# The last slot of an attention and convolution kernel: second pointwise layer and guides of one block as seven block products

## Chip, cores and metric

The kernel runs on one core of one Trainium2 chip. The metric is the device time of one execution in microseconds (us). TensorE (PE) multiplies matrices into PSUM, VectorE (DVE) does elementwise work and reads PSUM, ScalarE (ACT) does exponentials, GELU and copies, GpSimd (POOL) does small elementwise work, SyncE (SP) issues most DMAs.

## What is computed

The input x is 4 images of 64 x 64 pixels with 256 channels, float32. Layer 0 is full self-attention over the 4096 pixels of an image. Layer 1 is convolutional, cut to what matters here:

```python
perceived = depthwise_conv3x3(x, w_perc) + b_perc            # 256 -> 768 channels
hid = gelu(perceived @ w_up1.T + b_up1)                      # first pointwise layer, 768 -> 512
h   = x + hid @ w_up2.T + b_up2                              # second pointwise layer, 512 -> 256
q, k, v = split(h @ w_qkv.T + b_qkv)
scores = q . k over the 3 x 3 neighbours / 16
out = h + sum(softmax(scores) * v over the 3 x 3 neighbours)
```

The scores are formed without q and k: with G = Wq Wk (folded at the start), each pixel's "guide" is `g = G h + b`, and a score is `g . h` of the neighbour.

## The kernel before

**Slots and blocks.** An image is cut into 8 blocks of 8 rows (512 pixels); 4 images give 32 blocks. Slot s (0 to 31) does layer 0's attention of block s: 16 points (`points`, line 1091), each with one 1024-wide exponential on ACT (`weight`), four acc matmuls on PE (`product`, line 323, P times V), and one 1024-wide addition of the softmax denominator on DVE (`add_up`, line 337). At every even point PE also makes the next energies (`energy`, line 304, shown as e). Layer 1 follows behind: slot s also does the depthwise taps of block s − 2 and the pointwise layers, guides and scores of block k = s − 3, and the output of block a = s − 5. The last slot, 31, has more: k + 1 = 29 is done as well as k = 28, and the taps of blocks 29 and 30.

**The order** is written out by hand and each engine executes its instructions in that order. For every point: energies, the exponential, the jobs of `jobs[point]` (line 1129 in the last slot), `product`, `add_up`, and then a number of depthwise steps on DVE (`conv`, `tap_of` at line 477, one multiply-add of 128 x 512 each; the additions of line 483 make mixtures of the results). In the last slot these steps are spread evenly: 108 steps over 14 points, 7 or 8 each, with 20 at most by the end of point 2, so 11 in point 3. The first 60 belong to block 29 and end in point 7; its hidden layer (`hidden_part(k + 1, ...)`) starts in point 8.

**Seven products.** A product of a 2 x 2 block matrix with a 2 x 2 block matrix can be done with seven block products in place of eight, with additions before and behind (a Strassen form). The first pointwise layer does this for blocks 0 to 29 (`hidden_part`, tiles hid_a, hid_bc, hid_de, hid_gf). The second pointwise layer does it in `update_mix` (lines 669, 670: mixtures of hid), `update_part` (parts ab, cd, eg, f: 4 + 4 + 4 + 2 matmuls of 256 columns at line 534, with two DVE differences at lines 687 and 688 between ab and cd) and `gather` (lines 542 to 556: DVE adds each product into the result, ACT copies the first). Part f ends with four bias additions (line 698) and `guide_mix` (line 806). The guides do it in `guide_part` (2 + 2 + 2 + 1 matmuls, a DVE difference at line 833). The plain forms are `update(s, c)` (line 639, four matmuls of 512 columns, then two DVE operations at line 645, and with c = 1 the `border_terms`, lines 867 and 868) and `guide(s, i)` (line 783, two matmuls of 512 columns and one ACT operation at line 787).

Before, slots 3 to 30 use the seven products for update and guide; slot 31 uses the plain forms for blocks 28 and 29. The plain form of update needs the weights as they came, but the mixed weights stand in their place in `wup2`; so slot 31 starts with a DMA that loads that quarter again.

**PSUM banks.** A job takes its bank from `job_bank` (tag "m", two banks in turn): a job's first matmul waits until whoever reads the bank of the job before the previous one is done. Output tiles `o` have two buffers too; `lo` (block output, line 1029, with DVE at lines 1042 and 1054 and a DMA to HBM) and the two gmix tiles of `guide_mix` share them.

**The others in the slot:** `local_values` (lv, line 895, DVE 908), `scores` (s, line 936, ACT 956, POOL 961), `local_sum` (POOL 984), `local_total` (ld, line 998), `local_reciprocal` (DVE 1017), `border` (c, line 879). After slot 31 a tail starts with the denominators' matmul (dps, line 376) and does what is left of blocks 28 to 31.

## Time and profile before

| | us |
|---|---|
| time, median of 3 runs | 3453.34 (3453.23 to 3453.67) |
| the profiled execution, its own time | 3452.66 |
| its span, first to last instruction | 3450.8 |
| slot 31, from the dps before it (3199.97) to the dps behind it (3336.10) | 136.1 |
| the tail behind it | 114.7 |
| granted clock of TensorE | 0.999 |

The profile is one execution. "PE 3438.8 (100%)" is the busy time of an engine and its share of the span. The chain lists the work that ended last, followed back from the last instruction. A timeline row gives start, length, engine, line, operation, output <- inputs, how many were merged, and in brackets the idle time ahead of it and who ended it. A float32 matmul leaves two rows, so "x8" of 512 columns is four matmuls. Lengths of neighbouring rows overlap a little, so start to start is the better measure of cost.

### The profile page before, as it was taken

Reading aid. Unit: us, or ns where it says so; the run is one execution under the profiler, and the core shown is the slowest. Engines: PE = TensorE matmul, PEld = TensorE weight load, DVE = VectorE, ACT = ScalarE, POOL = GpSimd, SP = SyncE. Lnnn points to the kernel's source line nnn. Section 1 sums busy time; section 2 is a strip of 40 time slices with the busy share of each in tenths; the row PEclk is TensorE's granted clock in tenths of the full one; section 3 lists DMA queues with packets and bytes.
Section 4 is the critical chain, followed back from the end, with each engine's and each line's share of the span. In section 5 each row is a group of like instructions: output and inputs, shape, how many; then the busy total and the mean of one; then the engine's idle time right before and its main releaser. Section 6 shows DMA issues by size and latency. Waiting matters only on the chain.

```text
span 3450.8 us, 33708 instructions
## 1 busy us (share of the span) xinstructions
PE 3438.8 (100%) x12726; PEld 1994.8 (58%) x12726; DVE 2735.0 (79%) x4439; ACT 1063.9 (31%) x1328; POOL 359.2 (10%) x525
## 2 busy tenths in 40 slices
PE   9999999999999999999999999999999999999999
PEld 5445555556555556556555555566656555555555
DVE  2388888767888888876888888887688888888895
ACT  3232333323332233333333323333233333223331
POOL 2000001110111110111001111101110111110021
PEclk9999999999999999999999999999999999999999
DMA  4000000120000000011000000001100000000000
GB/s 107 7 4 10 7 10 16 28 48 18 16 14 9 16 16 16 22 25 46 16 10 16 10 13 16 16 22 30 42 16 16 16 10 7 16 16 18 7 7 26
DMA packets 93274, 67.05 MB, mean 19 GB/s; under 512 B 65872, under 2 KB 71248, under 8 KB 92976
## 3 DMA queue, kind: packets, MB, share of 16 engines
q1 hardware_dynamic: 92432, 64.42, 6.7%
q8 instruction: 102, 1.67, 0.2%
q14 instruction: 68, 0.56, 0.1%
q10 hardware_dynamic: 672, 0.39, 0.0%
HBM read 43.62 MB, written 18.81 MB: 18 GB/s over the span
## 4 chain that ended last, share of the span: by engine, by line
PE 98%; DVE 1%; DMA 0%; SPq 0%; ACT 0%; issue 0%; ACTq 0%; POOL 0%; DVEq 0%
PE acc L323 51%; PE e L304 8%; PE hid_de L582 5%; PE hid_gf L582 5%; PE hid_bc L582 5%; PE lv L895 3%; PE v L270 3%; PE lo L1029 3%; PE s L936 3%; PE hid_a L582 3%; PE dx_ab L534 2%; PE dx_cd L534 1%; PE dx_eg L534 1%; PE hid L614 1%; PE qk L236 1%; PE dx_f L534 1%
## 5 line engine op out<-in xcount | busy, mean ns | idle before, releaser
L323 PE MATMUL acc<-p,v 128*128 128x512 f32 x4096 | 1835.0, 594 | 0.3 <-DVE o L388 0.3
L323 PEld LDWEIGHTS acc<-p,v 128*128 128x128 f32 x4096 | 768.0, 190 | 809.9 <-issue 793.0
L477 DVE SCALAR_TENSOR_TENSOR perc<-xp,wperc,perc 128x512 f32<-128x512 f32 (+2 forms) x1554 | 1102.4, 770 | 27.5 <-ACT perc L473 27.3
L312 ACT ACTIVATE p<-e 128x1024 f32<-128x1024 f32 x512 | 524.0, 1024 | 1714.9 <-PE e L304 710.7
L337 DVE TENSOR_TENSOR den<-den,p 128x1024 f32<-128x1024 f32 x480 | 586.6, 1222 | 86.4 <-ACT p L312 84.7
L961 POOL TENSOR_TENSOR lp<-lp,near 128x396 f32<-128x396 f32 x60 | 96.3, 1604 | 2487.9 <-ACT lp L956 2487.9
L304 PE MATMUL e<-qa,ka 32*128 32x512 f32 x2048 | 292.0, 640 | 0.0
L304 PEld LDWEIGHTS e<-qa,ka 32*128 32x128 f32 x2048 | 80.0, 182 | 166.2 <-issue 145.3
L582 PE MATMUL hid_de<-perc,wmix 128*128 128x256 f32 x720 | 165.2, 379 | 0.0
L582 PEld LDWEIGHTS hid_de<-perc,wmix 128*128 128x128 f32 x720 | 136.8, 190 | 43.7 <-issue 21.5
L483 DVE TENSOR_TENSOR perc<-perc 128x256 f32<-128x256 f32 x360 | 153.4, 440 | 8.2
L605 ACT ACTIVATE hid<-hid,bup 128x512 f32<-128x512 f32 x120 | 80.1, 714 | 219.4 <-DVE hid L589 219.4
L473 ACT ACTIVATE perc<-xp,bperc,wperc 128x512 f32<-128x512 f32 x192 | 145.3, 805 | 1.7 <-DVE xp L394 1.7
L1029 PEld LDWEIGHTS lo<-lp,lv 128*128 128x128 f32 x732 | 102.9, 191 | 35.1 <-issue 27.3
L984 POOL TENSOR_TENSOR lsum<-lsum,lp 128x99 f32<-128x99 f32 x168 | 121.8, 731 | 11.0
L895 PE MATMUL lv<-wlv,h 128*128 128x256 f32 x520 | 122.4, 379 | 0.0
L589 DVE TENSOR_TENSOR hid<-hid_bc,hid 128x512 f32<-128x512 f32 x60 | 41.5, 692 | 101.9 <-PE hid_bc L582 101.9
L270 PE MATMUL v<-wv,xc 128*128 128x256 f32 x512 | 116.4, 380 | 0.3 <-DMA wv<-in_w_v 0.3
L270 PEld LDWEIGHTS v<-wv,xc 128*128 128x128 f32 x512 | 96.9, 190 | 28.5 <-issue 15.3
L936 PEld LDWEIGHTS s<-lq,h 128*128 128x128 f32 x520 | 87.1, 188 | 37.3 <-issue 27.4
L895 PEld LDWEIGHTS lv<-wlv,h 128*128 128x128 f32 x520 | 98.7, 190 | 15.5 <-issue 2.2
L1029 PE MATMUL lo<-lp,lv 128*128 128x99 f32 (+1 forms) x732 | 107.4, 295 | 0.0
(194 smaller groups left out, 3105.2 us busy)
## 6 DMA issues: line engine op xcount, KB each, us to landing
xp<-in_x SPq DMA_DIRECT2D x30, 528.0 KB, 4.0
xc<-in_x SPq DMA_DIRECT2D x56, 256.0 KB, 3.6
out<-lo SPq DMA_DIRECT2D x56, 256.0 KB, 2.0
qa<-packed SPq DMA_DIRECT2D x124, 64.0 KB, 2.0
out<-res SPq DMA_DIRECT2D x8, 256.0 KB, 2.0
ka<-st SPq DMA_DIRECT2D x124, 16.0 KB, 1.8
packed<-st SPq DMA_DIRECT2D x31, 64.0 KB, 1.9
wup<-in_w_up SPq DMA_DIRECT2D x1, 1536.0 KB, 6.5
```

The lines of the kernel that those rows point to most:

```text
L270: nc.tensor.matmul(ps[:, i * C : (i + 1) * C], lhsT=xc[:, kin, bass.ts(2 * pair + i, P)], rhs=wv[:, kin, :], start=(kin == 0), stop=(kin = ...
L304: nc.tensor.matmul(e[:, j, :], lhsT=key[rows, :], rhs=queries[s][rows, :], start=True, stop=True,)
L312: nc.scalar.activation(p, energies[s, G][:, 2 * half : 2 * half + 2, :], AF.Exp)
L323: nc.tensor.matmul(accs[s][c], lhsT=v[:, 2 * half + i, bass.ts(c, P)], rhs=p[:, i, :], start=(first and i == 0), stop=(G == NG - 1 and hal ...
L337: nc.vector.tensor_tensor(den, den, p, ALU.add)
L477: nc.vector.scalar_tensor_tensor(acc, win, wt, acc, ALU.mult, ALU.add)
L483: nc.vector.tensor_tensor(t[:, to, :], t[:, a, :], t[:, b, :], op)
L534: nc.tensor.matmul(ps[:, n * C : (n + 1) * C], lhsT=w(j), rhs=values(j), start=(j == 0), stop=(j == kin - 1),)
L582: nc.tensor.matmul(ps[:, n * C : (n + 1) * C], lhsT=w(j), rhs=mixes[s, j][:, kind, :], start=(j == 0), stop=(j == MULT - 1),)
L895: nc.tensor.matmul(ps[:, half * C : (half + 1) * C], lhsT=keys_of(s, t, half, kin), rhs=wlv[:, kin, :], start=(kin == 0), stop=(kin == CH ...
L936: nc.tensor.matmul(ps[:, t * QR * QW : t * QR * QW + rows * QW].rearrange("p (h w) -> p h w", w=QW), lhsT=keys_of(s, t, half, kin), rhs=gu ...
L1029: nc.tensor.matmul(pv[:, rows, columns(half)], lhsT=lvs[block, t, half][:, bass.ts(c, P)], rhs=near_ws[block, half][:, t, of, :], start=(i ...
```

## The change

In slot 31 block 28 gets `update_mix`, `update_part` and `guide_part` in place of `update` and `guide`, in points 3 to 8. The jobs behind them move: scores(28) from points 8 and 9 to 9 and 10, the second local_values(28) from 7 to 9, local_sum(27) from 9 to 10, local_total(27) and local_reciprocal(27) from 10 to 11, border_terms(28), which `update` did in point 5, to 10. Block 29's hidden parts stay in points 8 to 11 and its update stays plain, so the reload of the weights moves from the start of the slot to behind part f, in point 6.

```diff
+        def plain_update():
+            nc.sync.dma_start(out=wup2[:, :CH, P:], in_=w_up2[:, :CH, P:])
...
             if slot == NSLOT - 1:
-                nc.sync.dma_start(out=wup2[:, :CH, P:], in_=w_up2[:, :CH, P:])
                 jobs = [
                     job(hidden_part, k, 0, 0) + job(local_values, k - 1, 1),
                     job(local_denominator, a) + job(hidden_part, k, 0, 1),
-                    job(hidden_part, k, 1, 0), job(hidden_part, k, 1, 1) + job(local_product, a, 0),
-                    job(update, k, 0), job(update, k, 1) + job(local_product, a, 1),
-                    job(guide, k, 0) + job(local_values, k, 0),
-                    job(guide, k, 1) + job(local_values, k, 1),
-                    job(scores, k, 0) + job(hidden_part, k + 1, 0, 0),
-                    job(scores, k, 1) + job(local_sum, k - 1) + job(hidden_part, k + 1, 0, 1),
-                    job(hidden_part, k + 1, 1, 0) + job(local_total, a + 1)
+                    job(hidden_part, k, 1, 0),
+                    job(hidden_part, k, 1, 1) + job(local_product, a, 0) + job(update_mix, k),
+                    job(update_part, k, "ab"),
+                    job(update_part, k, "cd") + job(update_part, k, "eg") + job(local_product, a, 1),
+                    job(update_part, k, "f") + [plain_update],
+                    job(guide_part, k, "ab") + job(local_values, k, 0) + job(guide_part, k, "cd"),
+                    job(guide_part, k, "eg") + job(guide_part, k, "f")
+                    + job(hidden_part, k + 1, 0, 0),
+                    job(scores, k, 0) + job(local_values, k, 1) + job(hidden_part, k + 1, 0, 1),
+                    job(scores, k, 1) + job(local_sum, k - 1) + job(hidden_part, k + 1, 1, 0)
+                    + job(border_terms, k),
+                    job(hidden_part, k + 1, 1, 1) + job(local_total, a + 1)
                     + job(local_reciprocal, a + 1),
-                    job(hidden_part, k + 1, 1, 1), job(update, k + 1, 0) + job(border, k),
+                    job(update, k + 1, 0) + job(border, k),
                     job(local_product, a + 1, 0) + job(update, k + 1, 1),
                     job(local_product, a + 1, 1) + job(local_values, k + 1, 0),
                     job(local_values, k + 1, 1),
```

## The prediction

> **What bounds the kernel now.** I read the page's busy times and its chain first, then busy time by stretch, then the order of TensorE (PE) and VectorE (DVE) inside the last slot.

> ```profile
> PE 3438.8 (100%) x12726; PEld 1994.8 (58%) x12726; DVE 2735.0 (79%) x4439; ACT 1063.9 (31%) x1328; POOL 359.2 (10%) x525
> PE 98%; DVE 1%; DMA 0%; SPq 0%; ACT 0%; issue 0%; ACTq 0%; POOL 0%; DVEq 0%
> ```

> Over the whole span PE never rests. The change touches one slot only, number 31, some 136 us from 3200 to 3336 us. By stretch (us; busy PE, PEld, DVE, ACT, POOL; clock; DMA):

> ```profile
> 3200.00:3234.00 34.00, 34.00 (x145) 24.05 (x144) 27.14 (x45) 11.60 (x14) 0.57 (x2) 1.00 0.00 1
> 3234.00:3272.00 38.00, 38.00 (x129) 19.17 (x129) 37.15 (x65) 13.76 (x18) 0.00 (x0) 1.00 0.04 14
> 3272.00:3336.00 64.00, 64.00 (x233) 39.50 (x233) 54.79 (x87) 18.33 (x24) 12.35 (x21) 1.00 0.02 9
> ```

> In the middle stretch both engines are full: DVE works 37.15 of 38 us. This stretch holds points 4 to 7, where the changed jobs lie. The timeline at its end (start, length):

> ```profile
> 3269.50 1.68 DVE L483 TENSOR_TENSOR perc<-perc 128x256 f32<-128x256 f32 x4
> 3271.10 1.41 DVE L477 SCALAR_TENSOR_TENSOR perc<-xp,wperc,perc 128x512 f32<-128x512 f32 x2
> 3276.15 0.69 DVE L589 TENSOR_TENSOR hid<-hid_bc,hid 128x512 f32<-128x512 f32 x1 [3.65 <-PE hid_bc L582]
> ```
> ```profile
> 3270.55 1.61 PE L936 MATMUL s<-lq,h 128*128 128x198 f32 x8
> 3272.00 1.46 PE L582 MATMUL hid_a<-perc,wup 128*128 128x256 f32 x6
> ```

> DVE finishes the last mixture of block 29's depthwise outputs at 3271.2, and PE's first product of those outputs (hid_a, point 8) starts at 3272.0: 0.8 us of slack. Only after that does DVE wait again, 3.65 us. So DVE is the hidden second bound up to that product, and PE the bound after it.

> What the new form costs on DVE stands in slot 30, where the same functions run (lines 669 to 833):

> ```profile
> 3143.73 0.68 DVE L669 TENSOR_TENSOR hmix<-hid 128x512 f32<-128x512 f32 x1
> 3144.45 0.69 DVE L670 TENSOR_TENSOR hid<-hid 128x512 f32<-128x512 f32 x1
> ...
> 3148.18 0.68 DVE L687 TENSOR_TENSOR hid<-hmix,hid 128x512 f32<-128x512 f32 x1
> 3148.97 0.69 DVE L688 TENSOR_TENSOR hid<-hid 128x512 f32<-128x512 f32 x1
> 3149.58 0.42 DVE L546 TENSOR_TENSOR h<-dx_ab,h 128x256 f32<-128x256 f32 x1
> ...
> 3155.61 1.34 DVE L546 TENSOR_TENSOR h<-dx_eg,h 128x256 f32<-128x256 f32 x3 [0.84 <-PE dx_eg L534]
> ...
> 3161.52 1.67 DVE L698 SCALAR_TENSOR_TENSOR h<-h,bup,xp 128x256 f32<-128x256 f32 x4
> ```

> [...] 0.42 us for 256 columns, 0.69 us for 512. [...] halving a tile does not halve its DVE time, which is what makes seven products dear to gather. [...] the traces show both engines keep program order. [...]

> **The change, part by part.** Durations on DVE are start to start.

> PE: the update is now 14 matmuls of 256 columns (0.43 each: in slot 30 two of dx_cd take 0.86 us, 3151.96 to 3152.82) = 6.0 us for 3.63 + 3.43 = 7.06; the guides seven of them = 3.0 us for 1.92 + 1.72 = 3.64. Saved: 1.7 us. That is all there is to gain, since everything else on PE only changes place.

> DVE, up to the end of point 7's taps: update_mix 3143.73 to 3145.06 = 1.33; the two differences of L687/688 1.40; the gather of ab 0.33, cd 0.80, eg 1.26, f 0.34; four bias adds 1.70 for the two old pairs' 1.57 (3244.31 to 3245.09, 3250.79 to 3251.58), so 0.13; guide_mix 1.01; guide ab 0.40, its difference 0.33, cd 0.81. Added: 8.14. Moved out of this stretch: border_terms 0.80 (to point 10), the second local_values 0.67 (to point 9). Net 6.67. One new wait: in point 5 the product of block 26 (lo) needs the PSUM bank of cd, for there are only two such banks and every job takes the next one; it can start only after DVE has gathered cd, and takes 1.54 us, of which the eg gather hides about 1; I put 0.7 with the semaphores. Bounds 0 to 1.5. Nothing cancels this: DVE is in order and has no idle time there. Sum: 7.4 us later, so point 7's taps end at 3272.5 + 7.4 = 3279.9.

> Then hid_a. In the built order of the changed kernel g_eg and g_f stand ahead of it in point 8, and its bank is that of g_eg, so DVE's gather of eg and its biases (1.38, as 3173.79 to 3175.17) comes first: 3281.3, and 0.2 for the semaphore: 3281.5. Without stalls PE would be there at 3272.0 less 1.7 saved, less the first scores (1.54) and second values (1.73), which now come later: 3267.0. So PE loses about 14.5 us on the way. Where: at cd, which needs L687, which stands behind point 3's eleven taps (about 2.4); at lo for its bank (4); at guide ab, which needs the bias adds (1); at guide cd, whose bank waits for the ab gather behind point 6's taps (4.8); at hid_a (2.3). Their split does not matter: an early one only shortens a later one, since DVE's sum sets hid_a. Behind each stand the slot's acc products, so nothing overtakes.

> After hid_a PE needs what it needed, 3336.1 − 3272.0 = 64.1 us, plus the two jobs moved behind it (1.45 + 1.73): 3281.5 + 67.3 = 3348.8, against 3336.1. **Later by 12.7 us.** Does DVE keep pace there? Before, it was idle for 9.2 of these 64 us. Added: guide eg and f 1.4 + 0.4, border_terms 0.8, values 0.7, together 3.3, leaving about 9 in the longer stretch; so no lasting lag. The parallel taps ran 6.29 for 8 beside POOL's sum and 5.38 without; that moves by two points and may cost PE up to 0.7 at ld.

> Moves that I price at nothing: local_sum's POOL work (masking to the last add, 3281.4 to 3291.1) now has 12.6 us of PE work between scores and ld instead of 13.8, still 2 us more than it needs with the exponential; if POOL were 3 us slower, PE would wait 1. The weight reload (128 KB, 3.7 us to landing) goes past two output stores on SP and waits for f; its user, the second dx of block 29, comes at point 13, some 70 us later, and only stores of points 13 and 14 queue behind. Uncovered it would cost its 3.7 us. guide_mix takes the two buffers of lo's outputs; their stores land in 2.0 us and DVE gets there about 8 us later. border_terms is used two points later.

> The tail (3336 to the end) starts with PE and DVE in the same relation and keeps its order, so it shifts whole. Profiled span 3450.8 + 12.7 = 3463.5; that execution took 3452.66, 1.86 more than its span, and the median of the runs is 3453.34: forecast 3453.34 + 12.7 = 3466.0.

> **Rivals.**

> *PE stays the bound (not slower).* If DVE's taps in points 3 to 7 were not needed by hid_a, or DVE had spare time there, only PE's 1.7 us would count: 3451.6, within 0.2% of before. For it: page section 1, DVE 79%, and slot 30 runs the same forms with no PE gap. Against it: 37.15 of 38 us in that very stretch. It would need the taps themselves to be done sooner: with PE there at 3267.0, even a DVE without any added work lets hid_a start only at 3271.2, and PE ends at 3338.6, not earlier than before. So the point from which it decides is a hid_a at 3268.8 or before, 2.4 us under what DVE reaches today. 10%, for an error in how I read the dependence.

> *The stalls cool PE's clock.* [...] after the first gap DVE's lag hides it, after the second (guide cd, acc, then g_eg, on which hid_a hangs) it shows: about 3469.4. [...] 17%.

> *Fewer waits.* hid_a as soon as the mixtures are done (3271.2 + 6.7 = 3277.9), no bank wait: +9.1, 3462.4. Against: the bank order is fixed in the program. Part of the forecast's range.

> That the change doesn't act is excluded: the built order has the fourteen and seven matmuls in slot 31.

> **The numbers.** Forecast 3466.0, chance 70% (3462 to 3468); cool clock 17% (3468 to 3471); PE-bound 10% (3451 to 3453); something smaller, 3454 to 3461, 3%. The range takes the lower bound 3462.4 and the upper 3469.4 plus 0.7 of POOL: 3462 to 3470. A measurement can tell 0.2% (6.9 us) from no change: slower by more 0.87, within 0.12, faster 0.01.

> **What would show it.** Idle time of PE before dx_cd, the second lo, g_ab, g_cd and hid_a in slot 31, about 14 us in all, released by DVE; DVE with almost no idle time from point 4 to hid_a; the first dps of the tail 12 to 13 us later; the tail as long as before. It is wrong if PE shows gaps below 8 us there, if DVE idles between points 4 and 7, or if the delay arises after hid_a.

## The result, and the profile after

| | before | after |
|---|---|---|
| time, median of 5 runs (us) | 3453.34 (3453.12 to 3453.67) | 3470.34 (3470.02 to 3471.42) |
| span of the profiled execution | 3450.8 | 3468.1 |
| slot 31, dps to dps | 136.13 | 152.87 |
| of it, up to block 29's hid_a | 72.03 | 84.23 |
| of it, from hid_a on | 64.10 | 68.64 |
| tail behind it | 114.7 | 114.7 |

The changed kernel is slower by 17.0 us; the ratio is 1.005 (1.0039 to 1.0061). The forecast was 3466.0 with a range of 3462 to 3470: the direction is right, the time lies 0.34 us above the range. The profiled execution after started slot 31 0.58 us later than that of before, which is no part of the change.

The chain of the page after, and the three stretches of slot 31 (us; busy PE, PEld, DVE, ACT, POOL; clock; DMA):

```profile
PE 97%; DVE 2%; SPq 0%; DMA 0%; ACT 0%; issue 0%; ACTq 0%; POOL 0%; DVEq 0%
```
```profile
3199.97:3234.50 34.53, 34.53 (x145) 24.18 (x144) 27.14 (x45) 11.52 (x14) 0.57 (x2) 1.00 0.00 1
3234.50:3284.80 50.30, 40.01 (x132) 22.94 (x130) 45.70 (x81) 13.13 (x18) 0.00 (x0) 0.90 0.04 13
3284.80:3353.40 68.60, 67.51 (x248) 42.28 (x249) 56.36 (x93) 18.45 (x24) 11.61 (x21) 1.00 0.02 8
```

One point of the chain has gone from PE to DVE. The middle stretch is now 50 us long; PE works 40 of them, DVE 45.7, and the clock there is 0.90. The timeline of PE in it, with the one pause behind it (ld):

```profile
3246.96 1.30 PE L534 MATMUL dx_cd<-hid,wmix 128*128 128x256 f32 x4 [1.99 <-DVE hid L687]
3248.05 1.91 PE L534 MATMUL dx_cd<-hid,wup 128*128 128x256 f32 x4
3249.76 1.75 PE L534 MATMUL dx_eg<-hmix,wmix 128*128 128x256 f32 x4
3251.34 1.03 PE L534 MATMUL dx_eg<-hid,wmix 128*128 128x256 f32 x4
3254.68 3.32 PE L1029 MATMUL lo<-lp,lv 128*128 128x99 f32 x12 [2.31 <-DVE h L546]
3257.79 3.75 PE L323 MATMUL acc<-p,v 128*128 128x512 f32 x8
...
3274.83 1.85 PE L534 MATMUL g_cd<-gmix,gmix 128*128 128x256 f32 x4 [4.87 <-DVE lq L548]
3276.47 4.62 PE L323 MATMUL acc<-p,v 128*128 128x512 f32 x8
...
3284.78 1.56 PE L582 MATMUL hid_a<-perc,wup 128*128 128x256 f32 x6 [1.12 <-DVE lq L548]
...
3320.28 1.10 PE L998 MATMUL ld<-lsum,ones 128*128 128x512 f32 x2 [1.09 <-DVE hid L589]
```

In brackets are PE's pauses and who ended them: DVE each time. Four are places that the prediction named (g_ab, the fifth, did not pause, since PE came late); ld it had as a possible 0.7 us. But look at the lengths of the rows behind a pause: dx_cd's second pair takes 1.91 where the last dx_eg row shows 1.03 for the same shape; lo takes 3.32 for 1.70 in point 3; acc takes 4.62 for 3.60. Busy time of one microsecond each shows why (the clock is the third number from the end of a line):

```profile
3247.00:3248.00 1.00, 1.00 (x4) 0.89 (x5) 0.99 (x3) 0.49 (x1) 0.00 (x0) 0.90 0.00 0
3248.00:3249.00 1.00, 1.00 (x4) 0.77 (x3) 1.00 (x2) 0.00 (x0) 0.00 (x0) 0.50 0.00 0
3249.00:3250.00 1.00, 1.00 (x4) 0.82 (x3) 1.00 (x3) 0.00 (x0) 0.00 (x0) 0.50 0.00 0
3250.00:3251.00 1.00, 1.00 (x3) 0.77 (x3) 1.00 (x2) 0.00 (x0) 0.00 (x0) 0.50 0.00 0
3251.00:3252.00 1.00, 1.00 (x6) 0.85 (x4) 1.00 (x3) 0.00 (x0) 0.00 (x0) 0.89 0.00 0
```

After each of the first three long pauses PE ran at half clock for some 3.4 us. DVE in the same stretch:

```profile
3246.22 0.69 DVE L687 TENSOR_TENSOR hid<-hmix,hid 128x512 f32<-128x512 f32 x1
...
3254.45 1.33 DVE L546 TENSOR_TENSOR h<-dx_eg,h 128x256 f32<-128x256 f32 x3
3258.03 0.69 DVE L1042 SCALAR_TENSOR_TENSOR lo<-lo,lrden 128x512 f32<-128x512 f32 x1 [2.25 <-PE lo L1029]
...
3276.72 0.88 DVE L546 TENSOR_TENSOR lq<-g_cd,lq 128x256 f32<-128x256 f32 x2 [0.94 <-PE g_cd L534]
...
3280.09 1.68 DVE L483 TENSOR_TENSOR perc<-perc 128x256 f32<-128x256 f32 x4
3281.69 1.41 DVE L477 SCALAR_TENSOR_TENSOR perc<-xp,wperc,perc 128x512 f32<-128x512 f32 x2
3283.26 0.42 DVE L546 TENSOR_TENSOR lq<-g_eg,lq 128x256 f32<-128x256 f32 x1 [0.16 <-PE g_eg L534]
```

Ahead of hid_a DVE waits for PE in just two places of weight, 2.25 us at lo and 0.94 us at g_cd: PE waits for DVE, comes back at half clock, and now DVE waits for the product that is slow.

### The profile page after: what moved, and what is told of

Read it like the earlier page. It is cut to its first block, busy times and chain, and to the rows that moved or that the text cites. A ratio compares the mean times of both kernels' runs of the same rounds, so it can differ in the third digit from the quotient of the medians.

```text
span 3468.1 us, 33765 instructions
## 1 busy us (share of the span) xinstructions
PE 3444.7 (99%) x12744; PEld 2001.4 (58%) x12744; DVE 2745.7 (79%) x4461; ACT 1064.1 (31%) x1328; POOL 359.4 (10%) x525
## 3 DMA queue, kind: packets, MB, share of 16 engines
q8 instruction: 102, 1.67, 0.2%
## 4 chain that ended last, share of the span: by engine, by line
PE 97%; DVE 2%; SPq 0%; DMA 0%; ACT 0%; issue 0%; ACTq 0%; POOL 0%; DVEq 0%
PE acc L323 50%; PE e L304 8%; PE hid_bc L582 4%; PE hid_gf L582 4%; PE hid_de L582 4%; PE lv L895 3%; PE lo L1029 3%; PE v L270 3%; PE s L936 3%; PE hid_a L582 3%; PE dx_ab L534 2%; PE dx_cd L534 1%; PE dx_eg L534 1%; PE hid L614 1%; DVE perc L477 1%; PE g_eg L534 1%
## 5 line engine op out<-in xcount | busy, mean ns | idle before, releaser
L477 DVE SCALAR_TENSOR_TENSOR perc<-xp,wperc,perc 128x512 f32<-128x512 f32 (+2 forms) x1554 | 1102.6, 771 | 27.6 <-ACT perc L473 27.4
L582 PE MATMUL hid_de<-perc,wmix 128*128 128x256 f32 x720 | 165.2, 379 | 0.0
L582 PEld LDWEIGHTS hid_de<-perc,wmix 128*128 128x128 f32 x720 | 136.8, 190 | 43.8 <-issue 21.5
L483 DVE TENSOR_TENSOR perc<-perc 128x256 f32<-128x256 f32 x360 | 153.5, 440 | 8.2
L589 DVE TENSOR_TENSOR hid<-hid_bc,hid 128x512 f32<-128x512 f32 x60 | 41.5, 692 | 104.1 <-PE hid_bc L582 104.1
L936 PEld LDWEIGHTS s<-lq,h 128*128 128x128 f32 x520 | 87.1, 188 | 37.3 <-issue 27.4
```

The lines of the kernel that those rows point to most:

```text
L477: nc.vector.scalar_tensor_tensor(acc, win, wt, acc, ALU.mult, ALU.add)
L483: nc.vector.tensor_tensor(t[:, to, :], t[:, a, :], t[:, b, :], op)
L582: nc.tensor.matmul(ps[:, n * C : (n + 1) * C], lhsT=w(j), rhs=mixes[s, j][:, kind, :], start=(j == 0), stop=(j == MULT - 1),)
L936: nc.tensor.matmul(ps[:, t * QR * QW : t * QR * QW + rows * QW].rearrange("p (h w) -> p h w", w=QW), lhsT=keys_of(s, t, half, kin), rhs=gu ...
```

## The experiments

The theory after this: (1) DVE's work ahead of hid_a sets hid_a, as predicted; (2) PE's pauses halve its clock, and the two products that DVE waits for then take twice as long; (3) the moved border terms hold ld up. Rivals: the new order or the two PSUM banks cost by themselves; the half clock is hidden behind DVE; the cost goes with the number of products. Each was timed in 5 rounds beside the kernel before, whose median in those rounds was 3452.71 (e1 to e4), 3453.02 (e5 to e7) and 3452.97 (e8, e9).

| | us | over before | ratio (95%) |
|---|---|---|---|
| e1 the new order, plain forms | 3453.92 | 1.2 | 1.0004 (0.9995 to 1.0012) |
| e2 only the update in seven | 3462.58 | 9.9 | 1.0029 (1.0018 to 1.0041) |
| e3 only the guides in seven | 3462.18 | 9.5 | 1.0028 (1.0017 to 1.0038) |
| e4 changed, PE kept busy | 3467.13 | 14.4 | 1.0042 (1.0028 to 1.0055) |
| e5 before, more DVE work | 3459.39 | 6.4 | 1.0019 (1.0012 to 1.0027) |
| e6 changed, fewer taps | 3454.89 | 1.9 | 1.0005 (0.9997 to 1.0013) |
| e7 changed, hid_a first | 3469.53 | 16.5 | 1.0046 (1.0032 to 1.0060) |
| e8 changed, taps and block 29 later | 3471.72 | 18.8 | 1.0056 (1.0043 to 1.0070) |
| e9 changed, e4 + e7 + border terms later | 3464.62 | 11.7 | 1.0034 (1.0022 to 1.0046) |

The intervals of e1 and e6 include 1; but each of their runs is slower than every run of before beside it.

**e5: the suspected load alone, in the kernel before.**

```diff
+        def load(n):
...
+            for _ in range(n):
+                nc.vector.tensor_tensor(loads[0], wup1[:, 0, :], wup1[:, 1, :], ALU.add)
...
-                    job(update, k, 0), job(update, k, 1) + job(local_product, a, 1),
+                    job(update, k, 0) + [lambda: load(3)],
+                    job(update, k, 1) + job(local_product, a, 1) + [lambda: load(3)],
...
```

The results of these additions are not used; points 6 and 7 get load(3) and load(2) in the same way, behind `guide` and the values.

> The kernel before, with eleven additions of 128 x 512 on VectorE whose result is not used (3, 3, 3 and 2 in points 4 to 7, about 7.4 us); PE's work unchanged. Theory: VectorE has no room there, so hid_a moves from 3272.0 to about 3278.8: 6.8 us over before, 3460.1 (3459 to 3463, the upper part if PE's clock falls in the gaps). Rival (VectorE's added work is absorbed, the seven products cost in another way): 3453 to 3455.

Measured: 6.4 us over before. The timelines of PE and of DVE, and the same taps in the kernel before:

```profile
3273.06 1.13 PE L582 MATMUL hid_a<-perc,wup 128*128 128x256 f32 x4 [0.46 <-DVE lv L908]
3277.27 0.70 PE L582 MATMUL hid_a<-perc,wup 128*128 128x256 f32 x2 [3.08 <-DVE perc L477]
3277.81 2.55 PE L582 MATMUL hid_bc<-perc,wup 128*128 128x256 f32 x6
```
```profile
3276.28 1.80 DVE L477 SCALAR_TENSOR_TENSOR perc<-xp,wperc,perc 128x512 f32<-128x512 f32 x2
3278.11 1.68 DVE L483 TENSOR_TENSOR perc<-perc 128x256 f32<-128x256 f32 x4
```
```profile
3268.06 1.40 DVE L477 SCALAR_TENSOR_TENSOR perc<-xp,wperc,perc 128x512 f32<-128x512 f32 x2
```

hid_a starts on the two groups that are ready and stops 3.08 us for the third, ended by the first of the two taps. It runs before the four mixtures (line 483) have begun: hid_a reads no mixture (line 595 takes the plain part, LOWER). So the kernel before had more room than 0.8 us: there this tap ended at 3268.80 and the third group ran at 3272.86, some 4.1 us later.

Counted from the slot's dps, the tap ends 8.6 us later in e5 (about 7.4 us of additions; the last operations also ran longer than before, these two taps 1.80 us for 1.40, with POOL busy 4.5 of the 6 us from 3272 to 3278). The third group runs only 4.6 us later and hid_bc 4.7: the room took up the rest. Then hid_bc, behind the pause, takes 4.27 us start to start for 2.59 before, for the clock is at half from 3278.0 to 3281.4. 4.7 and 1.7 make the 6.4 us. So the rival was right for some 4 us of DVE's work, which is absorbed, and falls for the rest. That the total came near the expected 6.8 is luck: the larger room was nearly made up by the slower operations and the half clock.

**e6: the load taken away, in the changed kernel.** This kernel leaves out 20 taps of block 29.

```diff
                 elif tap > 0:
-                    tap_of(i, tap, *rows)
+                    if not (s == NSLOT - LAG_HID and tap > 3 and i % MULT):
+                        tap_of(i, tap, *rows)
                     yield
```

> The changed kernel with part of the computation left out: 20 of the 48 taps of block 29 (taps 4 to 8 of the second and third of its three output groups), 13.3 us of VectorE work in points 3 to 7; everything else as in the changed kernel. Theory: without the backlog the change costs almost nothing: hid_a near 3268.5, 3452 to 3455. Rival (the costs are the banks and the order, not VectorE's sum): most of the delay stays, 3463 or more.

Measured: 1.9 us over before. PE's pauses in slot 31 (line, who ended it, us in total, times, longest; its lines stand one lower):

```profile
PE hid_a L583 <- DVE lq L549: 1.1, 1, 1.1
PE ld L999 <- DVE hid L590: 1.1, 1, 1.1
```

The same order, the same banks, the same twenty-one products: the pauses at dx_cd, lo and g_cd are gone. So the banks at those three places cost only while DVE is behind. Two pauses stay: hid_a's bank, and ld.

**e1: the order alone.**

```diff
-                    job(hidden_part, k, 1, 1) + job(local_product, a, 0) + job(update_mix, k),
-                    job(update_part, k, "ab"),
-                    job(update_part, k, "cd") + job(update_part, k, "eg") + job(local_product, a, 1),
-                    job(update_part, k, "f") + [plain_update],
-                    job(guide_part, k, "ab") + job(local_values, k, 0) + job(guide_part, k, "cd"),
-                    job(guide_part, k, "eg") + job(guide_part, k, "f")
-                    + job(hidden_part, k + 1, 0, 0),
+                    job(hidden_part, k, 1, 1) + job(local_product, a, 0),
+                    job(update, k, 0),
+                    job(update, k, 1, False) + job(local_product, a, 1),
+                    [],
+                    job(guide, k, 0) + job(local_values, k, 0),
+                    job(guide, k, 1) + job(hidden_part, k + 1, 0, 0),
```

(False leaves the border terms to point 10; the reload is at the start again.)

> The changed order of jobs in the last slot (scores, values, sums, border terms one or two points later), but with the plain update and plain guides. Theory (VectorE's added work ahead of hid_a sets the time): VectorE loses 1.5 us of work ahead of hid_a and gains none, PE reaches hid_a some 3.3 us earlier and waits for the mixtures until about 3270; then 67.3 us of PE work as in the changed kernel: about 1 us over the kernel before, 3454.5 (3453 to 3456). Rival (the new order itself costs, through the sum on GpSimd or the banks): a large part of the 17 us appears here, 3460 or more.

Measured: 1.2 us over before, as the theory's number; but the place was another. hid_a did not wait, and started before the last mixture of line 483 was done (3267.61 to 3269.29). The one pause is at ld:

```profile
3268.50 1.46 PE L582 MATMUL hid_a<-perc,wup 128*128 128x256 f32 x6
```
```profile
3303.88 1.10 PE L998 MATMUL ld<-lsum,ones 128*128 128x512 f32 x2 [1.09 <-DVE hid L589]
```

So the moves cost 1.1 us, all at ld: border_terms now stands on DVE ahead of the gather that frees ld's bank. The sum after hid_a was therefore short by this in every variant with the new order: 68.5 to 68.6 us in e1, e2, e3, e4 and e6 for the predicted 67.3.

**e2 and e3: one form each.** e2 takes e1's two guide lines into the changed kernel and leaves guide_mix out for this block; e3 takes e1's update lines, with `job(guide_mix, k)` in point 6 for `[]`.

> The changed kernel with only the update in seven products; guides plain, guide_mix left away for this block. Theory: VectorE's net added work ahead of hid_a is 4.1 us and the wait for the lo product about 2.2 us (half clock) stays; hid_a needs no gather of guide parts. hid_a near 3277.7, then 67.3 us and up to 1 us at ld: 9 to 10 us over before, about 3463 (3461 to 3465). Rival (cost is spread evenly over the seven-product forms by their matmul count, 14 of 21): 3464.7; rival (guides alone cost): 3454.

> The changed kernel with only the guides in seven products, the update plain, guide_mix as a job of its own in point 6. Theory: VectorE's net added work ahead of hid_a is 1.1 us, a wait for g_cd about 0.9, and the gather of eg ahead of hid_a with two taps about 2.8; hid_a near 3276, then 67.3 us: 7 to 8 us over before, about 3461 (3459 to 3463). Rival (cost by matmul count, 7 of 21): 3459; rival (update alone costs): 3454.5.

Measured: 9.9 and 9.5 us over before. e2's profile has 6.2 us behind its last DVE instruction where e1 and e3 have 4.7; this stands outside the slot and its cause is open. In the slot itself, dps to dps, e1 takes 1.4 us more than before, and on top of that e2 adds 7.3 and e3 8.3, together 15.6 of the 15.4 that the whole change adds. So the costs of the two forms add up, the seven guide products cost no less than the fourteen update products, and the rival by number of products (2 to 1) falls. e3 lies in the upper half of the theory's range. In e2 hid_a does not wait at all: its cost stands at dx_cd (1.99) and lo (2.31) and in the half clock behind them. In e3 PE pauses at g_cd and at hid_a, and g_cd takes 2.08 for the 1.13 of slot 30:

```profile
3266.31 2.08 PE L534 MATMUL g_cd<-gmix,gmix 128*128 128x256 f32 x4 [4.52 <-DVE lq L548]
...
3277.09 1.56 PE L582 MATMUL hid_a<-perc,wup 128*128 128x256 f32 x6 [1.12 <-DVE lq L548]
```

One pause by DVE's backlog is enough to bring the half clock, 3264.6 to 3271.5 us here; e2 has it from 3247.1 to 3250.5 and from 3253.9 to 3257.4. Each form brings it by itself.

**e4: PE kept busy in the pauses.** Matmuls on constants whose results are not used: two ahead of dx_cd in its own bank, four ahead of lo and five ahead of g_cd in the energies' banks, which are free then.

```diff
+        def fill(ps, n):
+            for _ in range(n):
+                nc.tensor.matmul(ps, lhsT=ones, rhs=wup1[:, 0, :], start=True, stop=True)
...
-                    job(update_part, k, "cd") + job(update_part, k, "eg") + job(local_product, a, 1),
+                    job(update_part, k, "cd") + job(update_part, k, "eg")
+                    + [lambda: fill_e("fill_lo", 4)] + job(local_product, a, 1),
...
-                    job(guide_part, k, "ab") + job(local_values, k, 0) + job(guide_part, k, "cd"),
+                    job(guide_part, k, "ab") + job(local_values, k, 0)
+                    + [lambda: fill_e("fill_cd", 5)] + job(guide_part, k, "cd"),
```

> The changed kernel with matmuls whose results are not used (constant operands) put where PE would wait: two ahead of dx_cd, four ahead of the second lo, five ahead of g_cd. Theory (three waits let PE's clock fall to half, and the work behind them that VectorE waits for takes twice as long): no slice at half clock in the slot, VectorE's waits at lo and g_cd fall from 2.3 and 0.9 us to 0.7 and near 0, 2 to 3 us faster than the changed kernel: about 3467.8 (3466.5 to 3469). Rival (the half clock is hidden behind VectorE anyway): 3470.3 as the changed kernel, or later if the added matmuls are in the way.

Measured: 14.4 us over before, 2.6 less than the changed kernel's 17.0 (each against its own runs of before). The timeline of PE (its lines stand up to nine further down):

```profile
3249.71 3.60 PE L531 MATMUL fill_lo<-wup,ones 128*128 128x512 f32 x8
3253.86 1.77 PE L1038 MATMUL lo<-lp,lv 128*128 128x99 f32 x12 [0.56 <-DVE h L554]
3267.45 4.46 PE L531 MATMUL fill_cd<-wup,ones 128*128 128x512 f32 x10
3272.48 1.13 PE L542 MATMUL g_cd<-gmix,gmix 128*128 128x256 f32 x4 [0.58 <-DVE lq L556]
3281.46 1.56 PE L590 MATMUL hid_a<-perc,wup 128*128 128x256 f32 x6 [1.85 <-DVE lq L556]
```

lo takes 1.77 and g_cd 1.13 again, no stretch from 3244 to 3336 us shows a clock below 1.00, and hid_a starts 81.7 us behind the slot's dps; the prediction, at full clock, had 81.5 (3281.5 less 3199.97). DVE's waits fall to 0.7 us at lo and 0.2 at g_cd. PE does eleven matmuls more and the kernel is faster. That the clock is what cost 2.6 us is shown.

**e7: hid_a ahead of the last guide parts.**

```diff
-                    job(guide_part, k, "eg") + job(guide_part, k, "f")
-                    + job(hidden_part, k + 1, 0, 0),
+                    job(hidden_part, k + 1, 0, 0)
+                    + job(guide_part, k, "eg") + job(guide_part, k, "f"),
```

> The changed kernel with point 8's jobs in another order: hid_a and hid_bc ahead of the last guide parts, so that hid_a does not wait for the bank that VectorE frees when it has gathered guide eg. Theory: hid_a starts when the mixtures are done and the energies are through, about 3282.1 in place of 3284.8: 2 to 3 us faster than the changed kernel, 3467.8 (3466.8 to 3469). Rival (later waits eat it: scores need the guides, VectorE waits for hid_bc first): as the changed kernel, 3470.3.

Measured: 16.5 us over before, 0.5 less than the changed kernel, with runs from 3467.34 to 3470.19: a miss. hid_a does start earlier,

```profile
3282.73 1.56 PE L582 MATMUL hid_a<-perc,wup 128*128 128x256 f32 x6
...
3286.72 0.59 PE L534 MATMUL g_eg<-gmix,gmix 128*128 128x256 f32 x2
3287.15 0.59 PE L534 MATMUL g_eg<-h,gmix 128*128 128x256 f32 x2
3287.74 0.70 PE L534 MATMUL g_f<-gmix,wg 128*128 128x256 f32 x2
```

but g_eg and g_f, which used to fill PE while it waited, now come behind it and take 1.5 us to the next acc. The start of one product was the wrong mark; the pause (1.12) was the most to be had. With runs that spread by 2.9 us, the 0.5 itself is not clear of noise.

**e8: room for the gathers.** Fewer taps in points 3 to 7, block 29's hidden parts in points 10 to 13.

```diff
-                    to = min(n_steps, -(-(point + 1) * n_steps // (points - 2)))
+                    to = late_share[point]      # 8 16 20 25 28 33 36 41 49 60 72 84 96 108 ...
...
```

(The comment gives the steps done by the end of points 0 to 13. The jobs of points 8 to 15 move too: scores and the second values go ahead of block 29's hidden parts, its update goes to point 14.)

> The changed kernel with fewer taps beside the seven products (25, 28, 33, 36, 41, 49, 60 steps done by the end of points 3 to 9, then 12 a point) and block 29's hidden layer two points later (10 to 13), with scores and values ahead of it and its update in point 14. Theory (a gather waits behind the taps queued ahead of it): the waits at dx_cd and lo go, g_cd about 1, and what is left is hid_a, which VectorE's sum still keeps until about 3286 while PE has 12 us more of other work ahead of it: in all about 5 us over before, 3458 (3455 to 3461), no half clock. Rival (the two PSUM banks alone set the waits, whatever the taps): 3466 or more.

Measured: 18.8 us over before: a miss by 14 us, though the first half went as expected: dx_cd and the lo of point 5 do not wait at all, g_cd 0.91. So the banks alone do not set these waits, although the total lies in that rival's range. Then:

```profile
3287.07 0.70 PE L582 MATMUL hid_a<-perc,wup 128*128 128x256 f32 x2 [3.36 <-DVE perc L477]
...
3303.80 1.10 PE L998 MATMUL ld<-lsum,ones 128*128 128x512 f32 x2 [3.14 <-DVE hid L589]
...
3326.61 3.32 PE L1029 MATMUL lo<-lp,lv 128*128 128x99 f32 x12 [4.18 <-DVE hid L589]
```
```profile
3317.77 7.63 DVE L477 SCALAR_TENSOR_TENSOR perc<-xp,wperc,perc 128x512 f32<-128x512 f32 x12
3325.32 0.68 DVE L589 TENSOR_TENSOR hid<-hid_de,hid 128x512 f32<-128x512 f32 x1
```

The taps that were taken out of the first half stand in the second, twelve a point, 7.6 us ahead of every gather; and the half clock is there again behind 4.18. DVE's debt was only moved. My expectation had counted PE's and DVE's sums for points 10 to 13 as about equal and taken that for enough.

**e9: the three gains together.** e4 and e7, with border_terms behind the reciprocal in point 11 in place of point 10.

> The changed kernel with the matmuls that keep PE's clock up, hid_a ahead of the last guide parts, and border_terms behind the reciprocal in point 11. Theory: gains add up: 2.6 for the clock (measured), about 1.1 for hid_a's gap, 1.1 for the wait at ld that VectorE's border terms cause: 4.8 less than the changed kernel, 12.2 over before, 3465.3 (3464 to 3466.7). Rival (each gap that is closed opens the next): 3467 as with the clock alone.

Measured: 11.7 us over before, 5.3 less than the changed kernel for 4.8 expected; PE's pauses in the slot are down to 0.6, 0.6, 0.4 and 0.3, and ld does not wait. The gains add; that of border_terms was not timed alone. What is left is DVE's own added work, hidden under matmuls that do nothing. No version beat the kernel before; what one could gain is, by the prediction's own sum, the 1.7 us of matmuls saved.

## Why the prediction was wrong

**What held.** The bound and its place in the changed kernel: DVE full from point 4 to the gather that frees hid_a's bank, and PE the bound behind it (e4, e6). The net DVE work, 6.67 us: point 7's taps end at 3283.1, less 0.58 for the later start 3282.5, against 3272.5 before, so 10.0 later; less DVE's two waits of 2.25 and 0.94 that is 6.8. The gather ahead of hid_a, 1.4 and the semaphore. The tail shifts whole (114.7 both). The moves of the reload and of guide_mix's buffers cost nothing that shows.

**The step that failed** is the new wait: "I put 0.7 with the semaphores. Bounds 0 to 1.5", and none at g_cd. It took PE's products at full clock. DVE waited 2.25 us at lo, since lo took twice its time (3.32 for 1.70), and 0.94 at g_cd. 3.2 for 0.7: 2.5 us of the miss, and e4 gives 2.6 back when the clock is kept up; its wait at lo is then the 0.7 that was priced. The prediction had this as a rival with 17% and about 3469.4, 3.4 us over the forecast. How large the loss is and how long PE must pause for it were not shown by the trace of before (clock 0.999, no pause of PE in slot 31): the time was the author's estimate. Here pauses of 1.99 and 2.31 us were enough, in windows of 3.413 us in which PE worked 42% and 34% of the time (last section): no window had to be idle throughout, and three pauses cooled the clock, where the prediction priced one. The size was off as well: 3.4 us at half clock cost 1.7 us in e5 (hid_bc 4.27 us for 2.59). That the time fell into this rival's range of 3468 to 3471 is in part luck, for it put the loss at twice that and left out the wait at ld.

**The second term** is that after hid_a: 67.3 predicted, 68.6 measured. "may cost PE up to 0.7 at ld" left out that border_terms, priced by their 0.80 us in point 5, now stand ahead of point 10's taps and so of the gather that frees ld's bank, and run beside POOL there: 3311.3 to 3313.1, 1.8 us for the same four operations. PE waited 1.09 (e1, e9).

Together 2.7 us up to hid_a (84.2 for 81.5) and 1.3 behind it make 4.0 of the 4.3 us between forecast and result; the other 0.3 is not placed. The upper end of the range was made of the clock rival's 3469.4 and 0.7 at ld; with two causes of the same direction, each taken at its mild size, it missed by 0.34.

**A reading that was wrong without harm to the sum.** The prediction took the four mixtures as what hid_a needs, and so 0.8 us of slack before. hid_a needs a tap that ends 2.4 us ahead of the last mixture, with some 4.1 us of room (e5), and in e1 it started 0.8 us before the last mixture was done. The forecast did not suffer, since in the changed kernel hid_a waits for the gather of g_eg, which stands behind the mixtures in DVE's order. The bound of 3462.4 for fewer waits did rest on it.

**The rival on the other side** (PE stays the bound) fell, but not as argued, for its argument leaned on that same reading. What the runs show against it are PE's pauses, each ended by DVE, and e6: with 13 us of DVE work gone the changed kernel comes within 1.9 us of before, 1.1 of it at ld.

## What to carry to other kernels

Here 1.7 us of matmuls saved came with 17.0 us lost, since the vector engine had no time for the additions; whether it has is read in the stretch up to the product that needs its results, not from its 79% of the span. In the changed kernel pauses of the matmul engine of 1.99, 2.31 and 4.87 us were each followed by 3.4 us at half clock (one of 1.99 in e7 was not): with pauses of that length, cost what comes next at half clock as well, and first of all those products that the other engine waits for (lo took 3.32 us for 1.70). That one instruction starts shortly behind another doesn't show that it needed it: look up what it reads before the gap is called slack. Work that is moved later must be looked for again in front of the next gather: in e8 PE's and DVE's sums for points 10 to 13 had been counted as about equal, and the gather behind the 4.18 us pause stood behind 7.6 us of taps.

## What the runs showed of the hardware

| a window of 3.413 us at | PE busy in it | the next window |
|---|---|---|
| full clock, 11 windows | 2 to 41.8% | half clock |
| full clock, all others | 43.5% and more | full clock |
| half clock, 4 windows (e3, e7 twice, e8) | 45 to 75% | half clock again |
| half clock, 11 windows | 98.5 to 100% | full clock |

So in these traces a pause counted by its share of a window: the changed kernel's 1.99 us lay in one window (42% busy), e7's was cut by the edge of two (71 and 70%), e8's 3.14 likewise (64 and 43.5%). The half clock lasted one window, or two (6.8 us) where part of the pause reached into the first. An estimate from 43.5%: one pause of less than 1.9 us would have cooled no window of slot 31 by itself. Busy time is not the whole measure: in the tail, with its small products, windows of 51.5 and 52.5% were followed by half clock too (changed kernel, before). Where the windows lay against the program differed from trace to trace (one begins 43.8 us behind the slot's dps in the changed kernel, 42.0 in e7), and the runs of the changed kernel and of e7 spread by 1.4 and 2.9 us where those of before spread by 0.6 and 1.2 beside them. That this is where the spread comes from was not tested.

- DVE beside POOL: four operations of 8 columns took 0.80 us start to start alone (point 5 before) and 1.82 beside POOL's sum (point 10 after); eight taps 5.38 alone and 6.29 with POOL at work on the scores in 2.6 of them (lines 961 and 189; the prediction took it for the sum). That POOL's work is the cause was not shown: no run here took it away.
